# A contraction of 192 split into 128 rows and 64 rows, with the 64-row products of two pixel groups on two row groups of the array

## Chip, cores, metric

The kernel runs on one core of one Trainium2 chip. The metric is the device time of one execution in microseconds (us). Lower is better. Three different chips served the experiments, and the kernel before took 9693, 9727 and 9723 us on them, so kernels of different calls are compared by their ratio to the kernel before on the same chip.

## The reference

Two pre-activation convolution blocks on an image batch of 8 x 96 x 96 pixels and 192 channels, float32 throughout. The change touches only the dense part of the second block (layer 1):

```python
y = (y - mu) * lax.rsqrt(var + EPS) * ln_gamma + ln_beta   # layer norm over 192 channels
y = jnp.einsum('bhwc,cd->bhwd', y, w0) + b0                # 192 -> 768, first dense layer
y = jax.nn.gelu(y, approximate=False)
y = jnp.einsum('bhwd,dc->bhwc', y, w1) + b1                # 768 -> 192, second dense layer
return y * gamma                                           # gamma = 1e-6; added to x
```

## The kernel before

It has five passes. The last one, pass E, does the code above. Its unit of work is 4 pixel columns of 96 pixels, so 384 pixels; there are 192 units, loaded in 16 half images of 48 columns. A unit goes through a pipeline: statistics, norm, transposition, dense layers. The tools that build the kernel order each engine's instructions at build time; in the traces of before the instructions of VectorE, ScalarE and GpSimd start in the order of the built program (8406, 3840 and 1222 of them).

```python
    WE = 4
    # ... pools: ip bufs=2, sp bufs=3, tp bufs=2; PSUM: ps_t 2, ps_h 4, ps_o 2
        w0g = cp.tile([S, 2, EXP], F32, name="w0g")   # 192 rows of w0 as 2 x 96 (S = 96)
    # ...
        def transpose_e(yn):
            yT = tp.tile([S, 2, WE * S], F32, tag="yT", name="yT")
            for k in range(2):
                pt = ps_t.tile([128, WE * S], F32, tag="pt", name="pt")
                for j in range(WE):
                    nc.tensor.transpose(pt[:S, j * S : (j + 1) * S], yn[:, j, k * S : (k + 1) * S], ident[:S, :S])
                # ... copied out by ScalarE (k == 0) or VectorE (k == 1)
            return yT

        def layers_e(yT, r, n, w):
            g = tp.tile([128, NE, WE * S], F32, tag="g", name="g")
            for m in range(NE):                        # NE = 6 blocks of 128 outputs
                hp = ps_h.tile([128, WE * S], F32, tag="hp", name="hp")
                for k in range(2):                     # contraction 192 = 96 + 96
                    nc.tensor.matmul(hp, w0g[:, k, m * 128 : (m + 1) * 128], yT[:, k], start=(k == 0), stop=(k == 1))
                nc.scalar.activation(g[:, m], hp, AF.Gelu, bias=b0g[:, m : m + 1], scale=1.0)
            # ... second layer: po (2 columns a PSUM tile) <- g, w1g; VectorE adds the residual r:
            #     ot <- po, r; GpSimd adds the bias; store
```

Of the kernel before, what the change touches and what calls it, by code (L numbers as in the profile page):

```python
# [22 lines left out]
def rsqrt_eps(nc, pool, out, var, eps, neg_half, tag):  # L23
    """out = (var + eps) ** -0.5, by a tile of -0.5 at least as wide as out."""
    rows, n = out.shape
    t = pool.tile([rows, n], F32, tag=tag, name=tag)
    nc.vector.tensor_scalar(t, var, eps, None, ALU.add)
    nc.gpsimd.tensor_tensor(out, t, neg_half[:rows, :n], ALU.pow)  # L28


def group_stats(nc, pool, psum, piece, avg, neg_half):
    """Group norm of one image whose rows lie on the partitions.

    piece(g, i) is half i of group g. Gives steps to be emitted one after another, and a
    last one that returns [rows, 2, GROUPS] with 1/std and -mean/std on every partition."""
# [9 lines left out]
    def last():  # L45
        # Over the rows: the mean of the means, then that of var + (mean - its mean)^2.
        ps = psum.tile([128, 512], F32, tag="gn_ps", name="gn_ps")
        mean, var = ps[:rows, 0:GROUPS], ps[:rows, GROUPS : 2 * GROUPS]
        nc.tensor.matmul(mean, avg, mv[:, :, 0], start=True, stop=True)
        mean_sb = pool.tile([rows, GROUPS], F32, tag="gn_mean", name="gn_mean")  # L50
        nc.vector.tensor_copy(mean_sb, mean)
        d = pool.tile([rows, GROUPS], F32, tag="gn_d", name="gn_d")
        nc.vector.tensor_tensor(d, mv[:, :, 0], mean_sb, ALU.subtract)
        nc.vector.tensor_tensor(d, d, d, ALU.mult)
        nc.vector.tensor_tensor(d, d, mv[:, :, 1], ALU.add)
        nc.tensor.matmul(var, avg, d, start=True, stop=True)
        sh = pool.tile([rows, 2, GROUPS], F32, tag="gn_sh", name="gn_sh")
        rsqrt_eps(nc, pool, sh[:, 0, :], var, GN_EPS, neg_half, "gn_ve")
        nc.vector.scalar_tensor_tensor(
            sh[:, 1, :], mean_sb, -1.0, sh[:, 0, :], ALU.mult, ALU.mult  # L60
        )
        return sh
# [4 lines left out]
def load_bands(nc, out, z, c0, n_c, taps, size):  # L67
    """out[i, c, tap, j] = z[c0 + c, tap, i + j]: the taps' banded matrices, from input i to
    output size - 1 - j."""
# [10 lines left out]
def conv_blocks_kernel(  # L80
# [21 lines left out]
    """Two pre-activation convolution blocks, in five passes with float32 throughout:  # L102

    A  group norm and the projection D -> C, by image
    B  the 3x3 depthwise convolution and the running means, by channels, all images at once
    C  layer norm, the projection C -> D and the residual, by image; layer 1's statistics
    D  group norm and the 7x7 depthwise convolution, by channels, all images at once
    E  layer norm, the two dense layers with gelu and the residual, by image

    An image's C channels don't fit on chip, so what lies between two passes is in DRAM, in  # L110
    the order in which the next pass reads it."""
    nc = tc.nc
    B, S, _, D = x.shape  # images, side, channels
# [5 lines left out]
    GB = min(4, B)  # images side by side in one matmul  # L119
# [7 lines left out]
    P_d = dram.tile([C, B, S, S], F32, name="P_d")  # c, b, w, h  # L127
    M_d = dram.tile([S, C, B, S], F32, name="M_d")  # S - 1 - w, c, b, h
    X1_d = dram.tile([S, D, B, S], F32, name="X1_d")  # h, c, b, w
    Y_d = dram.tile([S, D, B, S], F32, name="Y_d")  # S - 1 - h, c, b, w  # L130
    Z0_d = dram.tile([C, 3, L], F32, name="Z0_d")  # c, kh, offset along w
    Z1_d = dram.tile([D, 7, L], F32, name="Z1_d")  # c, kw, offset along h
# [48 lines left out]
    with ExitStack() as ph:  # L181
# [31 lines left out]
        def columns(sh):  # L213
            """Scale and shift by channel, the channels on the partitions."""
# [89 lines left out]
    # Columns w on the partitions: kernel row kh is a banded matrix along w, and the shift  # L304
    # along h lies in the moving operand. The result lies in reverse order of w. The running
    # means along w are one matrix too, the same in either order.
    CC = 4
    with ExitStack() as ph:
# [7 lines left out]
        # The recurrence begins anew at each row.  # L316
# [5 lines left out]
        # mix = I + (running means along w, both ways) / 4, a symmetric matrix.  # L322
# [86 lines left out]
    WB = 6  # L409
    s1_pool = ExitStack()  # until the end of D  # L410
# [3 lines left out]
    with ExitStack() as ph:  # L414
# [8 lines left out]
        # (m - mean) * g @ W_out = m @ wc, wc = g * W_out less its column means.  # L423
        wc = cp.tile([128, NC, D], F32, name="wc")
        cst = cp.tile([S, D], F32, name="cst")  # ln_b @ W_out + b_out
# [28 lines left out]
        def load_c(b, w):  # L454
            """Columns w to w + WB; column w + j of M_d at WB - 1 - j."""
# [157 lines left out]
    WE = 4  # L613
    with ExitStack() as ph:
# [8 lines left out]
        w0g = cp.tile([S, 2, EXP], F32, name="w0g")  # gamma of the norm times w0  # L623
        w1g = cp.tile([128, NE, D], F32, name="w1g")  # w1 times the last gamma
        b0g = cp.tile([128, NE], F32, name="b0g")  # beta @ w0 + b0
        b1g = cp.tile([S, D], F32, name="b1g")  # b1 times the last gamma
        with tc.tile_pool(name="e_prep", bufs=1) as pp:
            nc.sync.dma_start(w0g, w0.rearrange("(k p) e -> p k e", p=S))
            nc.sync.dma_start(w1g, w1.rearrange("(m p) d -> p m d", p=128))
            gb = pp.tile([S, 2, 2], F32, name="gb1")  # L630
            b0s = pp.tile([128, NE], F32, name="b0s")
            with nc.allow_non_contiguous_dma(reason="one value per partition"):
                nc.sync.dma_start(gb[:, 0], ln_gamma.rearrange("(k p) -> p k", p=S))
                nc.sync.dma_start(gb[:, 1], ln_beta.rearrange("(k p) -> p k", p=S))
                nc.sync.dma_start(b0s, b0.rearrange("(m p) -> p m", p=128))
# [7 lines left out]
            for m in range(NE):  # L643
                for k in range(2):
                    nc.tensor.matmul(
                        ps[:, m : m + 1],
                        w0g[:, k, m * 128 : (m + 1) * 128],
                        gb[:, 1, k : k + 1],
                        start=(k == 0),
                        stop=(k == 1),  # L650
                    )
            nc.vector.tensor_tensor(b0g, b0s, ps[:, :NE], ALU.add)
            for k in range(2):
                nc.vector.tensor_scalar(
                    w0g[:, k], w0g[:, k], gb[:, 0, k : k + 1], None, ALU.mult
                )
# [3 lines left out]
        def load_e(n):  # L660
            b, half = divmod(n, 2)
            w = slice(half * HALF, (half + 1) * HALF)
            y = ip.tile([S, D, HALF], F32, tag="y", name=f"y_{n}")
# [15 lines left out]
        def norm_e(y, w, mv, rs):  # L679
            yn = sp.tile([S, WE, D], F32, tag="yn", name="yn", bufs=2)  # L680
            for j in range(WE):
                nc.vector.tensor_scalar(
                    yn[:, j],
                    y[:, :, w + j],
                    mv[:, j, 0:1],
                    rs[:, j : j + 1],
                    ALU.subtract,
                    ALU.mult,
                )
            return yn  # L690

        def transpose_e(yn):
            yT = tp.tile([S, 2, WE * S], F32, tag="yT", name="yT")
            for k in range(2):
                pt = ps_t.tile([128, WE * S], F32, tag="pt", name="pt")
                for j in range(WE):
                    nc.tensor.transpose(  # L697
                        pt[:S, j * S : (j + 1) * S],
                        yn[:, j, k * S : (k + 1) * S],
                        ident[:S, :S],  # L700
                    )
                # Rows h in their order again.
                src = pt[:S].rearrange("p (j h) -> p j h", j=WE)[:, :, ::-1]
                dst = yT[:, k].rearrange("p (j h) -> p j h", j=WE)
                if k == 0:
# [3 lines left out]
            return yT  # L709

        def layers_e(yT, r, n, w):
            g = tp.tile([128, NE, WE * S], F32, tag="g", name="g")
            for m in range(NE):
                hp = ps_h.tile([128, WE * S], F32, tag="hp", name="hp")
                for k in range(2):
                    nc.tensor.matmul(  # L716
                        hp,
                        w0g[:, k, m * 128 : (m + 1) * 128],
                        yT[:, k],
                        start=(k == 0),  # L720
                        stop=(k == 1),
                    )
                nc.scalar.activation(  # L723
                    g[:, m], hp, AF.Gelu, bias=b0g[:, m : m + 1], scale=1.0
                )
            ot = tp.tile([S, WE, D], F32, tag="ot", name="ot")
            for q in range(WE // 2):
                po = ps_o.tile([128, 2, D], F32, tag="po", name="po")
                for i in range(2):
                    j = q * 2 + i  # L730
                    for m in range(NE):
                        nc.tensor.matmul(  # L732
                            po[:S, i, :],
                            g[:, m, j * S : (j + 1) * S],
# [20 lines left out]
        for v in range(n_u + 3):  # L755
            if v < n_u:
                n, t = divmod(v, per)
                if t == 4 and n + 1 < 2 * B:
# [62 lines left out]
```

## Time and profile before

| | value | where from |
|---|---|---|
| time | 9694.13 us | median of 3 runs |
| pass E, TensorE busy | 1000 of 1000 us | stretch 8000 to 9000 us |
| pass E, first hp record to last matmul | 3121 us | starts of TensorE's records |
| of it first layer / second layer / transposes | 1496 / 1498 / 127 us | the same, summed |
| profiled span | 9721.9 us | the page |

The split in the fourth row is worked out from the trace: the time from each TensorE record's start to the next one's start is booked on the layer of the first (hp, po or pt). TensorE's listed ends are modelled and overlap, so only starts are added up. The profiled execution of before was slower than the timed ones (9721.9 against 9694.13 us), perhaps on another chip; pass E is compared by itself for that reason. The lines of the profile stand in the prediction below.

### The profile page before, as it was taken

How to read it: one execution, taken by the hardware profiler on the slowest of the kernel's cores; microseconds unless marked ns; L12 is line 12 of the kernel's file. 1: busy time of each engine (PE TensorE's matmuls, PEld its weight loads, DVE VectorE, ACT ScalarE, POOL GpSimd, SP SyncE). 2: the span in 40 equal slices, each digit the busy share in tenths (PEclk: the TensorE clock that was granted, in tenths of full speed). 3: DMA queues.
4: the chain of work that ended last, by engine and by line, in shares of the span. 5: the costliest groups of instructions: out<-in, count | busy, mean ns of one | idle time of the engine just before them, and what ended most of it. 6: DMA issues, size and time to landing. Idle time of an engine off the chain costs nothing.

```text
span 9721.9 us, 96185 instructions
## 1 busy us (share of the span) xinstructions
PE 8905.3 (92%) x37798; PEld 5953.8 (61%) x37798; DVE 4752.3 (49%) x8406; ACT 1962.9 (20%) x3842; POOL 2758.4 (28%) x1686
## 2 busy tenths in 40 slices
PE   6999999999998666656599999999999999999999
PEld 4666444444445555555455555547887777777777
DVE  5443899999997444444400000004444444444442
ACT  2333211111111111111111111112222222222222
POOL 1111233333334555554411111112222222222221
PEclk9999999999999888888899999999999999999999
DMA  6554555655554444554533333327334333433330
GB/s 176 180 180 151 140 133 133 142 133 138 135 133 118 129 124 126 139 134 117 126 97 90 94 98 98 98 80 94 53 48 63 56 54 48 63 55 55 48 48 19
DMA packets 1521772, 1008.28 MB, mean 104 GB/s; under 512 B 1443480, under 2 KB 1445801, under 8 KB 1499817
## 3 DMA queue, kind: packets, MB, share of 16 engines
q1 hardware_dynamic: 1457992, 605.44, 32.1%
q0 software_dynamic: 62720, 396.39, 12.3%
q8 instruction: 300, 4.92, 0.2%
q14 instruction: 152, 1.24, 0.0%
q10 hardware_dynamic: 608, 0.30, 0.0%
HBM read 603.77 MB, written 398.27 MB: 103 GB/s over the span
## 4 chain that ended last, share of the span: by engine, by line
PE 71%; POOL 8%; DMA 8%; DVE 2%; issue 1%; SPq 0%; ACT 0%; POOLq 0%; DVEq 0%; ACTq 0%
PE py L594 17%; PE po L732 15%; PE hp L716 15%; PE pl L351 15%; PE pa L374 5%; DMA xr<-in_x_dram 4%; POOL x1img L521 3%; POOL xr L504 3%; DMA mt<-M_d 3%; POOL rs L28 1%; PE pt L697 1%; DVE gn_st L42 1%; PE pm L254 1%; PE po L479 0%; POOL gn_sh L28 0%
## 5 line engine op out<-in xcount | busy, mean ns | idle before, releaser
L594 PE MATMUL py<-xn,band 96*96 96x372 f32 (+3 forms) x5376 | 1705.5, 480 | 32.1 <-POOL xn L579 32.1
L351 PE MATMUL pl<-pin,band 96*96 96x380 f32 (+1 forms) x4608 | 1541.0, 484 | 13.7 <-DMA pin<-P_d 13.7
L732 PEld LDWEIGHTS po<-w1g,g 128*96 128x96 f32 x9216 | 1497.7, 163 | 56.5 <-issue 30.6
L732 PE MATMUL po<-w1g,g 128*96 128x192 f32 x9216 | 1529.3, 326 | 0.0
L716 PE MATMUL hp<-yT,w0g 96*128 96x384 f32 x4608 | 1528.1, 488 | 0.3 <-ACT yT L706 0.3
L594 PEld LDWEIGHTS py<-xn,band 96*96 96x96 f32 x5376 | 874.6, 163 | 862.6 <-issue 726.0
L351 PEld LDWEIGHTS pl<-pin,band 96*96 96x96 f32 x4608 | 752.1, 163 | 742.9 <-issue 621.0
L716 PEld LDWEIGHTS hp<-yT,w0g 96*128 96x128 f32 x4608 | 862.5, 191 | 561.4 <-issue 3.0
L739 DVE TENSOR_TENSOR ot<-po,r 96x384 f32<-96x384 f32 x384 | 309.5, 806 | 1802.8 <-issue 1159.9
L370 POOL TENSOR_TENSOR both<-fw,bw 96x768 f32<-96x768 f32 x384 | 695.3, 1811 | 1283.6 <-DVE bw L366 1279.9
L364 DVE TENSOR_TENSOR_SCAN fw<-decay,loc 96x768 f32<-96x768 f32 x384 | 1049.6, 2733 | 18.6 <-ACT loc L359 18.6
L479 PE MATMUL po<-wc,mt 128*96 128x192 f32 x4608 | 947.3, 342 | 74.9 <-ACT xo L482 73.5
L745 POOL TENSOR_TENSOR ot<-ot,b1g 96x768 f32<-96x768 f32 x192 | 345.6, 1800 | 2193.7 <-DVE ot L739 2193.7
L576 DVE TENSOR_TENSOR xn<-xin,s 96x3072 f32<-96x3072 f32 x48 | 161.0, 3355 | 1502.7 <-PE py L594 1479.5
L723 ACT ACTIVATE g<-hp,b0g 128x384 f32<-128x384 f32 x1152 | 669.5, 581 | 903.7 <-PE hp L716 903.7
L473 DVE BATCH_NORM_STATS2 st<-pt 96x6 f32<-96x384 f32 x768 | 421.4, 555 | 843.1 <-PE pt L469 842.0
L479 PEld LDWEIGHTS po<-wc,mt 128*96 128x96 f32 x4608 | 750.9, 174 | 107.8 <-ACT xo L482 95.2
L254 PE MATMUL pm<-xT,win 96*128 96x384 f32 x2304 | 800.5, 498 | 0.0
L469 PE MATMUL pt<-ident,mt 128*96 128x128 f32 x2304 | 443.6, 291 | 386.8 <-DMA mt<-M_d 378.1
L359 ACT COPY loc<-pl 96x384 f32<-96x384 f32 x768 | 364.8, 475 | 1649.6 <-PE pl L351 1570.9
L366 DVE TENSOR_TENSOR_SCAN bw<-decay,loc 96x768 f32<-96x768 f32 x384 | 662.0, 1724 | 0.0
L254 PEld LDWEIGHTS pm<-xT,win 96*128 96x128 f32 x2304 | 432.5, 195 | 263.0 <-issue 18.0
(87 smaller groups left out, 6855.5 us busy)
## 6 DMA issues: line engine op xcount, KB each, us to landing
P_d<-po POOLq DMA_DIRECT2D x96, 1152.0 KB, 4.8
pin<-P_d SPq DMA_DIRECT2D x96, 1152.0 KB, 9.3
M_d<-mo POOLq DMA_DIRECT2D x96, 1152.0 KB, 6.0
mt<-M_d SPq DMA_DIRECT2D x384, 288.0 KB, 4.6
ximg<-in_x_dram SPq DMA_DIRECT2D x32, 1728.0 KB, 24.4
xr<-in_x_dram SPq DMA_DIRECT2D x128, 432.0 KB, 4.1
X_d<-x1img POOLq DMA_DIRECT2D x32, 1728.0 KB, 23.0
xin<-X_d SPq DMA_DIRECT2D x48, 1152.0 KB, 10.4
```

Source lines behind the costliest of these rows:

```text
L254: nc.tensor.matmul(pm, win[:, k, m * 128 : (m + 1) * 128], xT[:, k], start=(k == 0), stop=(k == 1),)
L351: nc.tensor.matmul(pls[g][:S, :, lo:hi], band[:, c, kh, :], pin[:, c, g * GB : (g + 1) * GB, lo + kh - 1 : hi + kh - 1], start=(n == 0), s ...
L364: nc.vector.tensor_tensor_scan(fw, decay_f, loc, 0.0, ALU.mult, ALU.add)
L366: nc.vector.tensor_tensor_scan(bw[:, ::-1], decay_f, loc[:, ::-1], 0.0, ALU.mult, ALU.add)
L370: nc.gpsimd.tensor_tensor(both, fw, bw, ALU.add)
L374: nc.tensor.matmul(pa[:S], mix, loc[:, g * GB * S : (g + 1) * GB * S], start=True, stop=True)
L469: nc.tensor.transpose(pt[:S, m * 128 : (m + 1) * 128], mt[:, m, WB - 1 - j, :], ident)
L479: nc.tensor.matmul(po[:S], mt[:, m, WB - 1 - j, :], wc[:, m], start=(m == 0), stop=(m == NC - 1))
L594: nc.tensor.matmul(pys[g][:S, :, lo:hi], band[:, c, kw, :], xn[:, b : b + GB, lo + kw - 3 : hi + kw - 3], start=(n == 0), stop=(n == 6),)
L716: nc.tensor.matmul(hp, w0g[:, k, m * 128 : (m + 1) * 128], yT[:, k], start=(k == 0), stop=(k == 1),)
L723: nc.scalar.activation(g[:, m], hp, AF.Gelu, bias=b0g[:, m : m + 1], scale=1.0)
L732: nc.tensor.matmul(po[:S, i, :], g[:, m, j * S : (j + 1) * S], w1g[:, m], start=(m == 0), stop=(m == NE - 1),)
```

## The change

Intent: a record over 128 rows takes no longer than one over 96. So 192 rows are split into 128 and 64 instead of 96 and 96. With two pixel groups at a time (8 columns a unit), the two products of 64 rows are placed on rows 0 to 63 and rows 64 to 127, to be multiplied at the same time. Four products per block of 128 outputs and two groups become two full ones and one pair: the first layer would take three quarters of its time. To make room, y and g get one buffer instead of two. Cut to its core:

```diff
-    WE = 4
+    WH = 4
+    WE = 2 * WH
+    DH = D - 128
...
-        w0g = cp.tile([S, 2, EXP], F32, name="w0g")
+        w0a = cp.tile([128, EXP], F32, name="w0a")
+        w0b = cp.tile([128, EXP], F32, name="w0b")     # the last 64 rows of w0, twice
...
-            y = ip.tile([S, D, HALF], F32, tag="y", name=f"y_{n}")
+            y = ip.tile([S, D, HALF], F32, tag="y", name=f"y_{n}", bufs=1)
...  (norm: the odd columns' channels are stored with the last 64 first, in two pieces)
...  (transposes: 8 of 128 channels into yA, 4 into yB, which holds 64 channels of an even
...   column on rows 0-63 and 64 of the odd column on rows 64-127; three PSUM tiles a unit, not two)
             for m in range(NE):
-                hp = ps_h.tile([128, WE * S], F32, tag="hp", name="hp")
-                for k in range(2):
-                    nc.tensor.matmul(hp, w0g[:, k, m * 128 : (m + 1) * 128], yT[:, k],
-                        start=(k == 0), stop=(k == 1))
+                e = slice(m * 128, (m + 1) * 128)
+                hps = [ps_h.tile([128, WH * S], F32, tag="hp", name="hp") for _ in range(2)]
+                for i in range(2):
+                    nc.tensor.matmul(hps[i], w0a[:, e], yA[:, i], start=True, stop=False)
+                for i in range(2):
+                    rows = slice(i * DH, (i + 1) * DH)
+                    nc.tensor.matmul(hps[i], w0b[rows, e], yB[rows], start=False, stop=True)
```

More of the change, by code (lines that the diff above doesn't have):

```diff
@@ L627, in conv_blocks_kernel @@
         with tc.tile_pool(name="e_prep", bufs=1) as pp:
-            nc.sync.dma_start(w0g, w0.rearrange("(k p) e -> p k e", p=S))
+            nc.sync.dma_start(w0a, w0[:128])
+            for i in range(2):
+                nc.sync.dma_start(w0b[i * DH : (i + 1) * DH], w0[128:])
             nc.sync.dma_start(w1g, w1.rearrange("(m p) d -> p m d", p=128))
-            gb = pp.tile([S, 2, 2], F32, name="gb1")
+            gb = pp.tile([128, 2, 2], F32, name="gb1")
             b0s = pp.tile([128, NE], F32, name="b0s")
             with nc.allow_non_contiguous_dma(reason="one value per partition"):
-                nc.sync.dma_start(gb[:, 0], ln_gamma.rearrange("(k p) -> p k", p=S))
-                nc.sync.dma_start(gb[:, 1], ln_beta.rearrange("(k p) -> p k", p=S))
+                for a, v in enumerate((ln_gamma, ln_beta)):
+                    nc.sync.dma_start(gb[:, a, 0:1], v[:128].unsqueeze(1))
+                    for i in range(2):
+                        nc.sync.dma_start(
+                            gb[i * DH : (i + 1) * DH, a, 1:2], v[128:].unsqueeze(1)
+                        )
                 nc.sync.dma_start(b0s, b0.rearrange("(m p) -> p m", p=128))
@@ L643, in conv_blocks_kernel @@
             for m in range(NE):
-                for k in range(2):
-                    nc.tensor.matmul(
-                        ps[:, m : m + 1],
-                        w0g[:, k, m * 128 : (m + 1) * 128],
-                        gb[:, 1, k : k + 1],
-                        start=(k == 0),
-                        stop=(k == 1),
-                    )
+                e = slice(m * 128, (m + 1) * 128)
+                nc.tensor.matmul(
+                    ps[:, m : m + 1], w0a[:, e], gb[:, 1, 0:1], start=True, stop=False
+                )
+                nc.tensor.matmul(
+                    ps[:, m : m + 1], w0b[:DH, e], gb[:DH, 1, 1:2], start=False, stop=True
+                )
             nc.vector.tensor_tensor(b0g, b0s, ps[:, :NE], ALU.add)
-            for k in range(2):
-                nc.vector.tensor_scalar(
-                    w0g[:, k], w0g[:, k], gb[:, 0, k : k + 1], None, ALU.mult
-                )
+            for k, t in enumerate((w0a, w0b)):
+                nc.vector.tensor_scalar(t, t, gb[:, 0, k : k + 1], None, ALU.mult)
         HALF = S // 2
@@ L681, in norm_e, with out_of @@
             for j in range(WE):
-                nc.vector.tensor_scalar(
-                    yn[:, j],
-                    y[:, :, w + j],
-                    mv[:, j, 0:1],
-                    rs[:, j : j + 1],
-                    ALU.subtract,
-                    ALU.mult,
-                )
+                parts = ((0, D, 0),) if j % 2 == 0 else ((0, 128, DH), (128, D, 0))
+                for lo, hi, to in parts:
+                    nc.vector.tensor_scalar(
+                        yn[:, j, to : to + hi - lo],
+                        y[:, lo:hi, w + j],
+                        mv[:, j, 0:1],
+                        rs[:, j : j + 1],
+                        ALU.subtract,
+                        ALU.mult,
+                    )
             return yn
         def transpose_e(yn):
-            yT = tp.tile([S, 2, WE * S], F32, tag="yT", name="yT")
-            for k in range(2):
-                pt = ps_t.tile([128, WE * S], F32, tag="pt", name="pt")
-                for j in range(WE):
-                    nc.tensor.transpose(
-                        pt[:S, j * S : (j + 1) * S],
-                        yn[:, j, k * S : (k + 1) * S],
-                        ident[:S, :S],
-                    )
-                src = pt[:S].rearrange("p (j h) -> p j h", j=WE)[:, :, ::-1]
-                dst = yT[:, k].rearrange("p (j h) -> p j h", j=WE)
-                if k == 0:
+            yA = tp.tile([128, 2, WH * S], F32, tag="yA", name="yA")
+            yB = tp.tile([128, WH * S], F32, tag="yB", name="yB")
+            ynf = yn.rearrange("p j d -> p (j d)")
+            def out_of(pt, dst, engine):
+                src = pt.rearrange("p (j h) -> p j h", j=WH)[:, :, ::-1]
+                dst = dst.rearrange("p (j h) -> p j h", j=WH)
+                if engine is nc.scalar:
                     nc.scalar.copy(dst, src)
@@ L708, in transpose_e @@
                     nc.vector.tensor_copy(dst, src)
-            return yT
+            for g in range(2):
+                pt = ps_t.tile([128, WH * S], F32, tag="pt", name="pt")
+                for j in range(WH):
+                    nc.tensor.transpose(
+                        pt[:, j * S : (j + 1) * S], ynf[:, (2 * j + g) * D + g * DH :][:, :128], ident[:S, :S]
+                    )
+                out_of(pt, yA[:, g], nc.scalar if g == 0 else nc.vector)
+            pt = ps_t.tile([128, WH * S], F32, tag="pt", name="pt")
+            for j in range(WH):
+                nc.tensor.transpose(
+                    pt[:, j * S : (j + 1) * S],
+                    ynf[:, 2 * j * D + 128 :][:, :128],
+                    ident[:S, :S],
+                )
+            out_of(pt, yB, nc.vector)
+            return yA, yB
         def layers_e(yT, r, n, w):
-            g = tp.tile([128, NE, WE * S], F32, tag="g", name="g")
+            yA, yB = yT
+            g = tp.tile([128, 2, NE, WH * S], F32, tag="g", name="g", bufs=1)
             for m in range(NE):
-                hp = ps_h.tile([128, WE * S], F32, tag="hp", name="hp")
-                for k in range(2):
-                    nc.tensor.matmul(
-                        hp,
-                        w0g[:, k, m * 128 : (m + 1) * 128],
-                        yT[:, k],
-                        start=(k == 0),
-                        stop=(k == 1),
-                    )
-                nc.scalar.activation(
-                    g[:, m], hp, AF.Gelu, bias=b0g[:, m : m + 1], scale=1.0
-                )
+                e = slice(m * 128, (m + 1) * 128)
+                hps = [ps_h.tile([128, WH * S], F32, tag="hp", name="hp") for _ in range(2)]
+                for i in range(2):
+                    nc.tensor.matmul(hps[i], w0a[:, e], yA[:, i], start=True, stop=False)
+                for i in range(2):
+                    rows = slice(i * DH, (i + 1) * DH)
+                    nc.tensor.matmul(hps[i], w0b[rows, e], yB[rows], start=False, stop=True)
+                for i in range(2):
+                    nc.scalar.activation(
+                        g[:, i, m], hps[i], AF.Gelu, bias=b0g[:, m : m + 1], scale=1.0
+                    )
             ot = tp.tile([S, WE, D], F32, tag="ot", name="ot")
@@ L733, in layers_e @@
                             po[:S, i, :],
-                            g[:, m, j * S : (j + 1) * S],
+                            g[:, j % 2, m, j // 2 * S : (j // 2 + 1) * S],
                             w1g[:, m],
@@ L757, in conv_blocks_kernel @@
                 n, t = divmod(v, per)
-                if t == 4 and n + 1 < 2 * B:
+                if t == 2 and n + 1 < 2 * B:
                     ins[n + 1] = load_e(n + 1)
```

## The prediction

In the prediction, hi and lo are names for the first and the second record of a product (24 records for 12 products a unit in the trace of before). "Drain" is its word for the delay of the first load after a change of row count, 0.22 us instead of 0.09 in stage A of that trace, at a granted clock of 0.54; what the array does in that time is not shown.

> **What bounds the kernel now.** I read the page first, then the busy time by stretches of the last stage, its groups of instructions, its timeline, and the waits. The change touches only the last stage (layer norm, the two dense layers, gelu), so what matters is what that stage waits for. The page's groups for its matmul lines:
>
> ```profile
> L732 PE MATMUL po<-w1g,g 128*96 128x192 f32 x9216 | 1529.3, 326 | 0.0
> L716 PE MATMUL hp<-yT,w0g 96*128 96x384 f32 x4608 | 1528.1, 488 | 0.3 <-ACT yT L706 0.3
> ```
>
> The column after the bar is busy time and mean; the last is idle time before. TensorE never waits here for another engine. The stretches of that stage (busy of each engine, then the granted clock and the DMA share) say the same:
>
> ```profile
> 8000.00:9000.00 1000.00, 1000.00 (x4934) 800.43 (x4933) 423.31 (x989) 243.36 (x430) 219.77 (x185) 1.00 0.38 54
> ```
>
> TensorE is busy 1000 of 1000 us at full clock, VectorE 423, ScalarE 243, GpSimd 220. So the stage costs what its TensorE instructions cost, one after another. One unit of the pipeline (4 pixel columns, 384 pixels) on the timeline of TensorE:
>
> ```profile
> 8005.04 0.83 PE L697 MATMUL pt<-ident,yn 96*96 96x96 f32 x8
> 8005.70 7.93 PE L716 MATMUL hp<-yT,w0g 96*128 96x384 f32 x24
> 8013.47 7.96 PE L732 MATMUL po<-w1g,g 128*96 128x192 f32 x48
> 8021.27 0.41 PE L697 MATMUL pt<-ident,yn 96*96 96x96 f32 x3
> ```
>
> The first column is the start. From starts alone: 0.66 us of transposes, 7.77 us of first layer (hp), 7.80 us of second layer (po), 16.23 us a unit; 192 units are 3116 us, a third of the kernel. The first layer is 12 float32 products a unit and 24 records: each product is two weight loads and two matmuls. One record takes 7.77/24 = 0.324 us from start to start; I call that a **slot** and use 0.3225 (the spacing in mid-stream). Its listed mean of 0.488 is the modelled end, which overlaps the next one.
>
> [...] two records per product, and 384 columns in 0.3225 us is 0.84 ns a column[...]. No row-packed pair runs in the kernel before. [...] stage A has products with one row next to full transposes, with no semaphore between them:
>
> ```profile
> 891.53 0.61 PE L222 MATMUL ps_col<-ident,row 1*96 1x1 f32 x3
> 891.62 0.43 PEld L222 LDWEIGHTS ps_col<-ident,row 1*96 1x96 f32 x2
> 892.07 0.24 PEld L238 LDWEIGHTS pt<-ident,ximg 96*96 96x96 f32 x2
> 892.08 0.40 PE L238 MATMUL pt<-ident,ximg 96*96 96x96 f32 x1
> ```
>
> Those small products start 0.16 us apart, and each next weight load starts 0.09 us after a product. The last of the three starts at 891.53 + 2 x 0.16 = 891.85, but the full-height load only at 892.07: 0.22 us later instead of 0.09. The three other places I looked at show 0.22 as well. The granted clock there is 0.54, so at full clock it will be less. [...]
>
> **The change, part by part.** A new unit is 8 columns, 96 units in all.
>
> *First layer.* Per 128 outputs and two groups of 384 pixels, before: 4 products, 8 slots = 2.58 us. After: two full products (4 slots) and two products of 64 rows on two row groups. The intent is that these two take the time of one: 6 slots. I do not believe 6. Each product is emitted as load hi, matmul hi, load lo, matmul lo, and the second product comes after the first. [...] The order is hi0, then lo0 beside hi1, then lo1: **three slots, not two**. If the load for hi1 is not pulled ahead of lo0, add about a weight load (the 96-column transposes start 0.083 us apart; scaled to 128 columns: 0.11 us), 3.34 slots.
>
> *Switches.* Every 128 outputs go from full rows to half rows and back: 2 switches, 12 a unit, 1152 in all. What one costs: the load, which the full stream hides behind a matmul, [...] (0.13 us late in the case above; 0.10 to 0.15 by my estimate at full clock), and then its own lead is open (0.03 to 0.11 us; after the transposes the first hp record starts 0.08 us after its load). I take 0.17 us, range 0.12 to 0.25. Per unit 12 x 0.17 = 2.04 us.
>
> *Transposes.* Before 16 of 0.083 = 1.33 us per 8 columns; after 12 of 128 columns, 12 x 0.11 = 1.32. But there are now three PSUM tiles through two buffers: the third waits for ScalarE's copy of the first. Four transposes 0.44, then 0.33 to the copy (before: 8005.29 to 8005.62), copy 0.475, so 1.2 us against 0.88 when the second group is through: 0.3 us a unit, 96 x 0.3 = 28 us.
>
> *Second layer.* Same products, same time. One buffer instead of two for g costs nothing[...].
>
> *Other engines.* VectorE normalizes in 12 pieces instead of 8 and still copies two tiles; its 6.9 us of 16.2 become some 14.6 of 32. ScalarE does the same gelus and one copy less. Neither becomes the bound.
>
> *Single buffer for y.* The next half image can be loaded only after the last norm of this one. The row of the DMA issues:
>
> ```profile
> y<-Y_d SPq DMA_DIRECT2D x15, 3456.0 KB, 26.1
> ```
>
> 26.1 us to land, then about 12 us of statistics and norm. When the last norm is done TensorE has some three units (3 x 32 us) of work in the pipeline, so the load fits. The danger is order: [...] if the statistics of the next image are queued before copies and residual adds of older units, a late load stops those. I give this 20 us in all (0 to 100).
>
> *Ends.* First statistics and norm of 8 columns instead of 4 (+6 us; TensorE waits 32.8 us there now), last residual, bias add (1.8 us becomes 3.6) and store: +15 us together.
>
> Sum per unit for three slots: 6 x (-0.3225) + 12 x 0.17 = -1.94 + 2.04 = +0.1 us, 96 x 0.1 = +10 us; with 28 + 20 + 15 = 63 us beside it, **+73 us: 9767 us**.
>
> **The rivals**, all with the same 63 us.
> - *3.34 slots* (load not pulled ahead): 6 x (-0.66 x 0.3225) + 2.04 = +0.76, +73 us; total +136: 9830. For it: in this trace a load always starts with the matmul before it, never earlier. [...] Weight 0.25; three slots have 0.40.
> - *No overlap at all* for float32 [...]: only the switches remain, +2.04 a unit, +196; total +259: 9953. Weight 0.22.
> - *Two slots*, as intended (records interleaved, or hi and lo of the two products paired in hardware): -3.87 + 2.04 = -1.83 a unit, -176; total -113: 9581. Without any drain it would be -371 + 63 = 9386. Weight 0.13.
> - *A buffer wait becomes the bound*: statistics waiting for y on VectorE and TensorE behind it. This would add to any of the above and show as 15 gaps, one for each half image.
>
> **Range and chances.** The weighted mean of the four is 0.40 x 73 + 0.25 x 136 + 0.22 x 259 - 0.13 x 113 = +106 us, 9800; the middle of the distribution lies lower. I say 9780. The drain moves each case by 12 x 96 x 0.06 = 70 us, so the range is 9590 to 9960. Faster by 2% means under 9500: two slots and a cheap drain, 0.09. Slower by 2% means over 9888: no overlap, or 3.34 slots with a dear drain or stalls on y, 0.27. Within 2%: 0.64.
>
> **What would show it right or wrong.** In the profile after: (a) starts of the 64-row records within one group: hi0, then lo0 and hi1 nearly together, then lo1 (three slots); lo0 and hi1 0.32 us apart would be no overlap. (b) At each change of row count the next load starts 0.1 us or more after the matmul before could have been followed, where it now starts 2 ns after a matmul's start. (c) The third transposed tile waits for the first copy. (d) VectorE waits on y, with or without TensorE idle behind it. I am wrong if the first layer's time per new unit falls clearly below 15.5 us, which is what two old units take now, or if TensorE shows idle time of more than 100 us in the stage.

## The result

The changed kernel took 9641.32 us (median of 4 runs, 9635.16 to 9645.75) against 9693.81 us. The ratio is 0.9944, 95% interval 0.9930 to 0.9958. Ratios here are the mean time of one kernel's fast runs over that of the other's of the same rounds, so not quite the ratio of the medians quoted. It is 52 us faster, where 86 us slower was forecast. The time lies in the range, but the sign is wrong.

TensorE's timeline over the first layer of one unit of 8 columns, after (start, length, engine, line, what; x is the count of records):

```profile
8007.98 0.83 PE L721 MATMUL pt<-ident,yn 96*128 96x96 f32 x8
8008.64 0.84 PE L742 MATMUL hp<-yA,w0a 128*128 128x384 f32 x2
8009.32 0.49 PE L727 MATMUL pt<-ident,yn 96*128 96x96 f32 x4
8009.65 0.84 PE L742 MATMUL hp<-yA,w0a 128*128 128x384 f32 x2
8010.42 0.92 PE L745 MATMUL hp<-yB,w0b 64*128 64x384 f32 x4
8011.26 1.56 PE L742 MATMUL hp<-yA,w0a 128*128 128x384 f32 x4
8012.75 0.92 PE L745 MATMUL hp<-yB,w0b 64*128 64x384 f32 x4
8013.60 1.56 PE L742 MATMUL hp<-yA,w0a 128*128 128x384 f32 x4
...
8022.93 8.04 PE L756 MATMUL po<-w1g,g 128*96 128x192 f32 x48
```

The four full records go from 8011.26 to 8012.75, 1.49 us: four slots (1.29) and 0.20. The four half records go from 8012.75 to 8013.60, 0.85 us: **two** slots (0.645) and 0.20. So the pair really takes the time of one, and each change of row count costs 0.20 us. The four half records start in two couples, at 8012.749 and 8012.756, then 8013.176 and 8013.182: the first records of both groups side by side, then the second ones. One block takes 2.34 us instead of 2.58. The third transposed tile does not hold TensorE up: two full records were placed before it.

Yet not all of that arrives. The waits of pass E after (engine and line, what it waited for: us in total, times, longest):

```profile
PE po L756 <- DVE ot L763: 79.0, 15, 6.8
DVE st L682 <- DMA y<-Y_d: 8.5, 8, 2.1
```

In the kernel before TensorE has no wait of the first kind. It now waits 15 times, once per half image but the first, for VectorE to free a po tile by the residual add. One such place on the timeline, VectorE and TensorE:

```profile
8030.25 5.42 DVE L682 BATCH_NORM_STATS2 st<-y 96x6 f32<-96x192 f32 x14
...
8035.58 1.49 DVE L763 TENSOR_TENSOR ot<-po,r 96x384 f32<-96x384 f32 x2
8036.41 10.09 PE L756 MATMUL po<-w1g,g 128*96 128x192 f32 x48 [5.45 <-DVE ot L763]
```

In square brackets stand the idle time before and what ended it. y had landed long before, at about 8011, and VectorE had been busy with statistics and norms of the new half image ever since. It took up the residual adds, for which two full po tiles had been waiting, only at 8035.58. TensorE stood for 5.45 us and then went on at half clock (0.50), as the stretch from 8035 to 8040 shows (the third number from the end is the granted clock):

```profile
8035.00:8040.00 5.00, 3.58 (x11) 3.22 (x12) 2.06 (x4) 0.00 (x0) 0.00 (x0) 0.50 0.00 0
```

Summed as before, from the starts (us; the kernels of the experiments stand below the line):

| kernel | first layer | second layer | transposes | pass E | ratio to before (95%) |
|---|---|---|---|---|---|
| before | 1496 | 1498 | 127 | 3121 | 1 |
| changed | 1348 | 1619 | 96 | 3063 | 0.9944 (0.9930 to 0.9958) |
| | | | | | |
| e1_pad | 1499 | 1577 | 96 | 3172 | 1.0060 (1.0047 to 1.0072) |
| e2_y2 | 1347 | 1507 | 96 | 2950 | 0.9838 (0.9824 to 0.9851) |
| e3_share | 1243 | 1643 | 96 | 2982 | 0.9866 (0.9852 to 0.9879) |
| e4_share_y2 | 1242 | 1503 | 96 | 2840 | 0.9721 (0.9708 to 0.9735) |
| e5_sep | 1258 | 1648 | 96 | 3001 | 0.9887 (0.9873 to 0.9900) |
| e6_before_y1 | 1495 | 1498 | 127 | 3120 | 1.0000 (0.9987 to 1.0014) |
| e7_onegroup | 1716 | 1522 | 96 | 3334 | 1.0225 (1.0211 to 1.0239) |
| e8_st2 | 1347 | 1539 | 96 | 2982 | 0.9866 (0.9852 to 0.9879) |
| e9_st1 | 1346 | 1506 | 96 | 2948 | 0.9834 (0.9821 to 0.9847) |
| e10_share_st1 | 1242 | 1519 | 96 | 2856 | 0.9744 (0.9731 to 0.9758) |

The changed kernel gains 148 us in the first layer and 32 us in the transposes and loses 121 us in the second layer, in which not one product changed. Of the 1348 us, 5.0 are a single wait of TensorE at the start of the pass, released by VectorE's copy of yA.

### The profile page after: what moved, and what is told of

Same layout as the page of the kernel before. It is cut to its first block, busy times and chain, and to the rows that moved or that the text cites. A ratio compares the mean times of both kernels' runs of the same rounds, so it can differ in the third digit from the quotient of the medians.

```text
span 9641.9 us, 94893 instructions
## 1 busy us (share of the span) xinstructions
PE 8756.8 (91%) x37414; PEld 5630.2 (58%) x37414; DVE 4730.2 (49%) x8694; ACT 1850.3 (19%) x3746; POOL 2620.2 (27%) x1398
## 4 chain that ended last, share of the span: by engine, by line
PE 65%; DMA 10%; POOL 8%; DVE 7%; issue 1%; SPq 0%; POOLq 0%; ACT 0%; DVEq 0%
PE py L594 18%; PE pl L351 15%; PE po L756 14%; PE hp L742 7%; PE pa L374 5%; PE hp L745 4%; DMA xr<-in_x_dram 4%; POOL x1img L521 3%; DMA mt<-M_d 3%; POOL xr L504 3%; DVE st L682 3%; DMA y<-Y_d 2%; POOL rs L28 1%; DVE gn_st L42 1%; PE pm L254 1%; DVE yn L694 1%
## 5 line engine op out<-in xcount | busy, mean ns | idle before, releaser
L756 PE MATMUL po<-w1g,g 128*96 128x192 f32 x9216 | 1556.2, 331 | 79.0 <-DVE ot L763 79.0
L769 POOL TENSOR_TENSOR ot<-ot,b1g 96x1536 f32<-96x1536 f32 x96 | 330.1, 3439 | 2192.9 <-DVE ot L763 2192.9
L742 PE MATMUL hp<-yA,w0a 128*128 128x384 f32 x2304 | 910.8, 511 | 0.0
L747 ACT ACTIVATE g<-hp,b0g 128x384 f32<-128x384 f32 x1152 | 605.7, 577 | 854.9 <-PE hp L745 854.9
L742 PEld LDWEIGHTS hp<-yA,w0a 128*128 128x128 f32 x2304 | 384.2, 190 | 389.9 <-issue 262.6
```

What stands on the lines that cost most here:

```text
L742: nc.tensor.matmul(hps[i], w0a[:, e], yA[:, i], start=True, stop=False)
L747: nc.scalar.activation(g[:, i, m], hps[i], AF.Gelu, bias=b0g[:, m : m + 1], scale=1.0)
L756: nc.tensor.matmul(po[:S, i, :], g[:, j % 2, m, j // 2 * S : (j // 2 + 1) * S], w1g[:, m], start=(m == 0), stop=(m == NE - 1),)
```

## The experiments

Two theories: (T1) the two row groups work at the same time, hi beside hi and lo beside lo, and each change of row count costs a fixed 0.2 us; (T2) the loss in the second layer comes from VectorE's order after the single-buffered y has landed. The rivals stand with each run. All results counted as correct, e7's as well, which is wrong on purpose: layer 1's dense part is multiplied by a gamma of 1e-6, so the comparison with the reference hardly sees it. It says nothing about the first dense layer of these kernels; that rests on how they are written.

**e1_pad: no row groups, no change of row count.**

```diff
-        w0b = cp.tile([128, EXP], F32, name="w0b")
+        w0z = cp.tile([128, 2, EXP], F32, name="w0z")   # group i's 64 rows, the others zero
+        nc.vector.memset(w0z, 0.0)
...  (w0z is loaded, and scaled by the norm's gamma, in place of w0b)
-                    nc.tensor.matmul(hps[i], w0b[rows, e], yB[rows], start=False, stop=True)
+                    nc.tensor.matmul(hps[i], w0z[:, i, e], yB, start=False, stop=True)
```

> The changed kernel, but the 64 rows of each group are multiplied at full height, with the other group's 64 weight rows set to zero: no row groups, no change of row count, the same products and data. Correct result. Theory (pairing gains two slots of 0.3225 us per 128 outputs and two groups, the two changes of row count cost 0.2 us each, so 0.245 us net): the first layer goes back to 8 slots, 2.58 us per 128 outputs instead of 2.33, so 576 x 0.245 = +141 us on the changed kernel, about 9780 us. Rival (the gain comes from elsewhere, such as fewer transposes or fewer units): within 30 us of the changed kernel.

Measured: 9750.25 us, ratio 1.0060. On TensorE's timeline the four records of the padded halves and the four full ones now follow one another with nothing between:

```profile
8002.51 1.45 PE L746 MATMUL hp<-yB,w0z 128*128 128x384 f32 x4
8003.80 1.45 PE L744 MATMUL hp<-yA,w0a 128*128 128x384 f32 x4
8005.09 1.45 PE L746 MATMUL hp<-yB,w0z 128*128 128x384 f32 x4
```

1.29 us each, four slots, so eight for a block. The first layer grows by 1499 - 1348 = 151 us, near the 141 expected. The time grew by about 110 us only, because the second layer shrank by 42 us (1619 to 1577): with a longer first layer VectorE has more time, and TensorE waits less for it (49.8 us in the 15 waits on residual adds, where the changed kernel has 79.0). Pairing is where the first layer's gain comes from; the rival falls.

**e7_onegroup: the changes of row count, but no pairing.**

```diff
-                    rows = slice(i * DH, (i + 1) * DH)
+                    rows = slice(0, DH)                 # wrong on purpose
```

> The changed kernel with both half products on rows 0 to 63, so the second pixel group is multiplied with the first one's rows: a wrong result on purpose; all instructions, counts and changes of row count as in the changed kernel. Theory (what the change gains is the overlap of the two groups, two slots each time): 576 x 2 x 0.3225 = +371 us on the changed kernel, about 10010 us, less what the waits on residual adds shrink (up to 40 us); the second product's first record starts 0.64 us after the first's. Rival (half products are faster by themselves, as fewer rows are streamed): under 100 us.

Measured: 9943.49 us, ratio 1.0225, so about 272 us slower than the changed kernel (1.0225 - 0.9944 = 0.0281 of 9694). The first layer grew by 1716 - 1348 = 368 us, where 371 was expected. The half records of one block:

```profile
8003.20 1.55 PE L745 MATMUL hp<-yB,w0b 64*128 64x384 f32 x4
8004.68 1.56 PE L742 MATMUL hp<-yA,w0a 128*128 128x384 f32 x4
```

1.48 us for the same four half records that took 0.85 us on two row groups. They are not faster by themselves; the rival falls. I had allowed 40 us for shrinking waits; the second layer shrank by 1619 - 1522 = 97 us, nearly all that it had lost, so the time missed the 10010 expected.

**e5_sep: four records of one group ahead of the other group's.**

```diff
+            for m0 in range(0, NE, 2):                  # two blocks at a time, four hp tiles
...                full products of both blocks and groups
                 for i in range(2):
                     rows = slice(i * DH, (i + 1) * DH)
+                    for a in range(2):
+                        nc.tensor.matmul(hps[a][i], w0b[rows, e], yB[rows], start=False, stop=True)
```

> The changed kernel with two blocks of 128 outputs taken together: four full products, then group 0's half product for both blocks, then group 1's for both. So in program order four records of group 0 stand ahead of the first of group 1. Theory (each row group works off its own records, and a record of the other group overtakes those that wait): the first record of group 1 starts within 0.02 us of the first of group 0, the eight records take 4 slots (1.29 us), time near that of the kernel with shared changes of row count, 9540 to 9620 us. Rival (matmuls start strictly in program order, and only what stands next to one another overlaps): group 1 starts with group 0's fourth record, some 0.97 us later, 7 slots, 3 x 0.3225 x 288 = +279 us on that, over 9800 us.

This asks why the pair takes two slots. The compiled TensorE program of the changed kernel holds hi0, lo0, hi1, lo1 in this order, as I had assumed. That of this kernel holds four load-and-matmul pairs of rows 0 to 63 and only then four of rows 64 to 127. Measured: 9616.06 us, ratio 0.9887.

```profile
8017.41 1.57 PE L751 MATMUL hp<-yB,w0b 64*128 64x384 f32 x8
8019.05 2.85 PE L746 MATMUL hp<-yA,w0a 128*128 128x384 f32 x8
```

The eight half records end after 1.57 us: in the trace they start in four couples, 8017.408 and 8017.421, then 8017.835 and .848, 8018.157 and .170, 8018.480 and .493. The first record of the other group overtook three that stood before it. Seven slots would have taken 2.26 us to the start of what follows; it started after 1.64. So these records did not start in program order across the row groups, and the rival, which was the prediction's step, falls.

**e3_share: half as many changes of row count.**

```diff
...  (full and halves: the two loops over i of the changed kernel, made functions)
+                # even blocks: full, halves; odd blocks: halves, full
+                for n_, part in enumerate((full, halves) if m % 2 == 0 else (halves, full)):
+                    part(m, hps, n_ == 0)               # start=(n_ == 0), stop=(n_ == 1)
```

> The changed kernel with the halves of two neighbouring blocks of 128 outputs next to each other (full, halves, halves, full), so 6 changes of row count per unit of 8 columns instead of 12. Theory (a change costs 0.2 us): 576 fewer x 0.2 = -115 us, about 9525 us. Rival (a change costs nothing by itself and the gap is the weight load's start): under 30 us.

Measured: 9562.23 us, ratio 0.9866, 76 us under the changed kernel (0.0078 of 9694). The first layer lost 1348 - 1243 = 105 us for 576 changes fewer, 0.18 us each; 115 was expected. The second layer gave 24 us back, since TensorE's waits on the residual adds grew:

```profile
PE po L763 <- DVE ot L770: 109.5, 15, 8.1
```

So a change has its price, and the rival falls. The two effects are not independent while VectorE's order stays: what the first layer saves, VectorE loses as time to catch up (waits of 109.5 us against 79.0). e1 and e7 show the same the other way round, with 49.8 and 13.4 us.

**e2_y2: two buffers for y.**

```diff
-            y = ip.tile([S, D, HALF], F32, tag="y", name=f"y_{n}", bufs=1)
+            y = ip.tile([S, D, HALF], F32, tag="y", name=f"y_{n}")
-            ot = tp.tile([S, WE, D], F32, tag="ot", name="ot")
+            ot = tp.tile([S, WE, D], F32, tag="ot", name="ot", bufs=1)
```

> The changed kernel with two buffers for y again, paid for by one buffer instead of two for ot. Theory (the single buffer for y makes VectorE catch up after each late load; TensorE then waits 15 times for residual adds, 79 us in the trace, and each wait is followed by some microseconds at half clock, about 50 us in all): the 15 waits vanish, the clock stays at 1.00, 110 to 140 us less, about 9515 us. Rival (the waits come from two buffers for po, or the clock falls because of the drains at the changes of row count): less than 30 us gained, the waits stay.

Measured: 9535.15 us, ratio 0.9838, 103 us under the changed kernel, a little less than the 110 to 140 expected. The wait is down to one, and the granted clock from 7000 to 9300 us is 1.00:

```profile
PE po L756 <- DVE ot L763: 2.3, 1, 2.3
```

The second layer falls from 1619 to 1507 us, 112 us: 79 us were waiting, and the other 33 can be added up in the changed kernel's trace: the records after the 15 waits start up to 0.32 us apart instead of 0.163, while the granted clock is 0.50. This makes the single y buffer a condition of the wait (the run also takes one of ot's two buffers; that this removes a wait is unlikely, but it was not tested alone), but doesn't yet show how.

**e6_before_y1: the single buffer in the kernel before.**

```diff
-            y = ip.tile([S, D, HALF], F32, tag="y", name=f"y_{n}")
+            y = ip.tile([S, D, HALF], F32, tag="y", name=f"y_{n}", bufs=1)
```

> The kernel before with one buffer for y instead of two and nothing else. Theory (the single buffer costs by itself, whatever the size of the unit: 15 late loads, each followed by a burst of statistics on VectorE that holds up the residual adds): 60 to 130 us slower, 15 waits of TensorE. Rival (the cost comes only with units of 8 columns): within 15 us of the kernel before.

Measured: 9727.00 us against 9727.35, ratio 1.0000. My theory that the single buffer costs by itself fell here. The late load and the run of statistics are there as well, but TensorE does not wait:

```profile
7946.26 3.58 DVE L673 BATCH_NORM_STATS2 st<-y 96x6 f32<-96x192 f32 x9
7949.75 0.79 DVE L739 TENSOR_TENSOR ot<-po,r 96x384 f32<-96x384 f32 x1
```

```profile
7940.55 7.97 PE L732 MATMUL po<-w1g,g 128*96 128x192 f32 x48
7948.35 0.83 PE L697 MATMUL pt<-ident,yn 96*96 96x96 f32 x8
7949.02 7.93 PE L716 MATMUL hp<-yT,w0g 96*128 96x384 f32 x24
7956.79 7.97 PE L732 MATMUL po<-w1g,g 128*96 128x192 f32 x48
```

A unit of 4 columns fills two po tiles and there are two buffers. The first residual add, due at 7944.5, came at 7949.75, but the next po tile is wanted at 7956.79, after the transposes and the first layer of the next unit. A unit of 8 columns fills four po tiles, so the third is wanted 7.8 us after the first was begun, within the same unit, and the run of statistics over columns of 8-column units is longer: from 8011 to 8035.6 in the changed kernel. Neither the single buffer alone (e6) nor the unit of 8 columns alone (e2) makes the wait; the two together do.

**e8_st2 and e9_st1: VectorE's order alone, y still single.**

```diff
-            st = sp.tile([S, WE, 6], F32, tag="st", name="st")
+            st = sp.tile([S, WE, 6], F32, tag="st", name="st", bufs=2)   # e9: bufs=1
-            mv = sp.tile([S, WE, 2], F32, tag="mv", name="mv")
+            mv = sp.tile([S, WE, 2], F32, tag="mv", name="mv", bufs=2)
-            rs = sp.tile([S, WE], F32, tag="rs", name="rs")
+            rs = sp.tile([S, WE], F32, tag="rs", name="rs", bufs=2)
```

Fewer buffers for the statistics keep them from being ordered far ahead. In both kernels the programs of TensorE, ScalarE and SyncE are the same as in the changed kernel; VectorE's order changes (and GpSimd's with it).

> The changed kernel with two buffers instead of three for the tiles of the statistics (st, mv, rs), y still single. TensorE's, ScalarE's and SyncE's programs are the same, instruction for instruction; only VectorE's order changes, and its run of statistics ahead of the residual adds gets shorter by one unit's eight columns, some 3.7 us. Theory (the run of statistics after each load of y holds up the residual adds, and TensorE, out of po buffers, waits): each of the 15 waits of some 5.3 us shrinks to about 1.6, 55 us less idle and some of the 30 us at half clock, 60 to 85 us less than the changed kernel. Rival (TensorE waits because y lands late): no gain, as y lands at the same time.

> As before with one buffer for st: the run ahead of the residual adds is two units' statistics and half of a third, some 10 us shorter than in the changed kernel; norms move as well. Theory: the waits on residual adds vanish, 95 to 115 us less than the changed kernel, as with two buffers for y, unless a norm now comes late. Rival: no gain.

Measured: e8 9593.53 us, ratio 0.9866, 76 us under the changed kernel; e9 9560.94 us, ratio 0.9834, 107 us under it. The waits of e8:

```profile
PE po L756 <- DVE ot L763: 24.2, 15, 2.7
DVE st L682 <- DMA y<-Y_d: 7.5, 8, 1.6
```

and of e9:

```profile
PE po L756 <- DVE ot L763: 0.3, 1, 0.3
```

A run of statistics shorter by one unit leaves 15 waits of 1.6 us (as worked out beforehand), one shorter by more leaves a single one of 0.3 us. The loads of y did not move: in the changed kernel, e8 and e9 alike each is issued 8.0 us after a unit's transposes start, and lands some 25 us later. That settles T2: it is the order on VectorE, not the landing of y. The extra memory of e2 is not needed.

**e4_share_y2 and e10_share_st1: the two cures together.**

> Both: shared changes of row count and two buffers for y. Theory: the two gains add, -115 and -130, about 9395 us, 3% under the kernel before. Rival (both touch the same idle time): less than three quarters of the sum.

> Shared changes of row count and one buffer for st, y still single. Theory: as fast as with two buffers for y and shared changes, ratio to the kernel before 0.972 to 0.976. Rival (the shorter first layer leaves VectorE too little time, and waits come back): 0.98 or more.

Measured: e4 9424.27 us, ratio 0.9721, faster than both kernels: 2.8% under the kernel before and 0.0223 of 9694 = 216 us under the changed kernel, more than the 103 + 76 of its parts. Most of the difference is that without T2's waits the second layer gives nothing of e3's gain back (24 us there). 216 us is less than the 245 expected, as a shared change saved 0.18 us and not 0.20, and the waits were worth 103 us and not 130. e10 reached 0.9744; the waits came back in small:

```profile
PE po L763 <- DVE ot L770: 17.5, 14, 1.9
```

Its edits are those of e3 with those of e2 (e4) or of e9 (e10).

## Why the prediction was wrong

- **"The order is hi0, then lo0 beside hi1, then lo1: three slots, not two."** This step failed and turned the sign. The program order was as assumed; that the records start strictly in it was an assumption that no trace had shown. The pair takes two slots (0.645 us and a change), and e5 shows records of one row group overtaking three of the other. The term was a gain of one slot, 576 x 0.3225 = 186 us; e7 measures two, 368 us.
- **Switches, 1152 x 0.17 = 196 us.** Nearly right in size; the traces show the delays, not what the array does in them. 368 us gained less the 148 us that are left make 220 us, 0.19 each (5 us of it are the wait at the start); e3 gives 0.18 and the timeline 0.20. Both parts of the term are in the trace: the first record after a change starts 0.41 us after the last one before it, instead of 0.3225, and the second one 0.43 us after the first, its weight load 0.108 us after the first load.
- **Transposes, +28 us.** Wrong in sign: they gained 32 us (127 to 96). The third tile does not wait, as two full records were placed before it, and transposes with 128 columns start 0.083 us apart like those with 96, not 0.11. The 4 saved ones make 96 x 4 x 0.083 = 32 us.
- **Single buffer for y, "20 us in all (0 to 100)".** The danger was named rightly (VectorE's order, residual adds held up, 15 gaps), but the term was mis-sized: 103 us (e2) to 107 us (e9) of the time, and 112 to 113 us in the second layer. What I had not seen is the po tiles: four per unit through two buffers, where before two per unit went through two (e6). The half clock after each wait I had not counted at all: in the changed kernel a stretch at 0.50 begins in the course of each of the 15 waits (4.63 to 6.80 us long), 14 of 6.83 us and one of 10.24. With shorter waits less of it was seen: from 6700 to 9300 us the mean granted clock is 0.98 there and 1.00 in e8, where TensorE waits 2.7 us at most for a residual add.
- **Ends, +15 us.** At the start some 10 us show, of which 6 were forecast: from the last matmul of the pass before to the first hp record 44.5 us go by instead of 40.0, and the wait of 5.0 us just after it is new. At the end nothing of the other 9 us shows: from the last matmul's start to the end of the span it is 13 us in both profiles.
- **Sum.** -368 + 220 - 32 + 113 = -67 us; pass E measures -58. The 8 or 9 us left are in the second layer, 1498 to 1506 us with the waits gone (e9): its first two records in each unit start 0.240 us apart instead of 0.167, 96 x 0.073 = 7 us, since they now follow a change of row count. In e1 and e4, where they follow a full product, it is 0.163.
- **The rivals.** "Two slots, as intended" was the right one, given 0.13. Its time, 9581, was 60 us under the result: the waits cost 93 us more than their 20 and the changes 24 us more than their 196, while the transposes came out 60 us better. That the forecast's range still holds the result is luck in part: the missed slot (182 us) and the missed waits (93 us) pull in opposite directions.
- "I am wrong if the first layer's time per new unit falls clearly below 15.5 us": it fell to 1348 / 96 = 14.0 us.

## What to carry to other kernels

A packed pair of half-height products paid two slots here against four on one row group (0.85 against 1.48 us, a change of row count included), but each change between full and half height cost 0.18 to 0.20 us, so put the halves of neighbouring blocks next to each other (76 us in e3). When a unit of work is doubled, count its tiles against every buffer, also of stages that do not change: here twice as many po tiles through two buffers turned a harmless late load into a wait, and the cure was to keep another engine's work from being ordered too far ahead. A saving on the bound engine shortens the time that the others have, and may come back as a wait (from 79.0 to 109.5 us in e3); look for it before blaming the saving.
